# Attention block with adaptive layer norm: the softmax's sums moved from the weights by key to the scores by query, blocks 4 to 15

## The chip, the cores and the metric

The kernel runs on one core of a Trainium2 chip. The metric is the device time of one execution in microseconds; the median of three runs is compared. The core has TensorE (PE, the matrix unit; its weight loads are a row of their own, PEld), VectorE (DVE), ScalarE (ACT), GpSimd (POOL) and SyncE (SP, which issues most DMAs). TensorE writes only to PSUM, eight banks of 512 float32 columns on 128 partitions.

## The reference

Eight sequences of 1024 rows, 512 wide, 16 heads of 32, all float32:

```
mod = silu(condition) @ Wada + bada          # six rows per sequence: shift, scale, gate, twice
xm = layernorm(x) * (1 + sc_a) + sh_a
q, k, v = split(xm @ Wqkv)
attn = softmax(causal(q @ k.T * hd**-0.5))   # sums over the keys
x = x + gt_a * (attn @ v @ Wproj + bproj)
xm = layernorm(x) * (1 + sc_m) + sh_m
x = x + gt_m * (gelu(xm @ W1 + b1) @ W2 + b2)
```

## The kernel before

The rows are cut into 16 blocks of 512, two per sequence: block n has h = n % 2, and the odd block attends to the keys of both. Heads are taken four at a time (a group, g = 0 to 3), one on each quarter of TensorE's rows or columns. The linear products (q, k, v, proj, up, down) use a scheme with seven products of half size for a product of four quarters; their operands' sums and differences run on VectorE and GpSimd.

Attention makes each score twice. **By query** (`scores`, L1828): the scores of a query tile of 128 rows go into the four-bank PSUM tile `sc`, the causal mask is added on VectorE (L1842), and VectorE takes the maximum of each row (L1845). Per group there are whole units of 512 keys and units on the diagonal: one of 512 columns, one of 384 and 128, one of twice 256 that two groups share. `split_maxima` cuts the maxima into three bfloat16 parts, and `maxima_rows` turns them into a row by small matmuls (L1883). **By key** (`weights_T`): the negative maximum (L1909, bfloat16) and the scores (L1921) are added up in the PSUM tile `st`, and ScalarE takes the exponential of 2048 elements at once (L1934) into `pT` in SBUF. `sc` and `st` are the same four banks: one buffer, so each use waits for the one before to be read. Three further banks serve all linear products (`bank`), and the last is `po`, the sum of weights times values (`weigh`, L1962).

The softmax's sums come from the weights by key: `add_weights` (L2047, GpSimd) adds the group's `pT` tiles up, and `finish` multiplies the total by a matrix of ones (L1983, TensorE), which gives each query's sum on all its rows. ScalarE takes the logarithm (L1993), copies `po` (L1996), takes the exponential of the negative logarithm (L2001), and VectorE or GpSimd multiplies.

What stands where in each engine's queue is decided when the program is recorded. A recorder keeps a clock for each engine from planned costs (`note`, `note_pe`, `note_act`) and due times of what is written and read. The linear products are generators; `step_aside` inserts their matmuls ahead of an attention step until the step's buffer is due to be free. `plan` lists the linear steps by window; `MANNER` has leanings for single groups. The chip then runs each queue in that order, with semaphores.

Of the kernel before, what the change touches and what calls it, by code (L numbers as in the profile page):

```python
# [22 lines left out]
def kernel(  # L23
# [252 lines left out]

    plan = {
# [7 lines left out]
    for w in range(1, NB):  # L285
# [167 lines left out]
    cond_act = tmp.tile([P, TB], F32, tag="top", name="cond_act", bufs=1)[:B, :]  # L453
# [939 lines left out]
    def down(n, part):  # L1393
# [77 lines left out]
        def key(kind):  # L1471
            return {"u1": "p1", "u3": "p1", "u5": "u4", "u2": "u2"}.get(kind) or y_key(kind)

        got = partials
        if part == 0:
# [3 lines left out]
            got["u1"] = stage("p1", "p1")  # L1479
# [3 lines left out]
            got["u5"] = stage("p5", "u4")  # L1483
# [23 lines left out]
        else:  # L1507
            u2, u5 = got["u2"], got["u5"]
            bank, ps = yield from product("B11")
            u3 = stage("u3", "p1")  # L1510
# [141 lines left out]
    def work():  # L1652
# [10 lines left out]
        done_linear[0] += spent[0] - before  # L1663
        run_jobs()
# [22 lines left out]
    def step_aside(reads, writes):  # L1687
# [12 lines left out]
        while BANK in writes and bank_at() == NEVER:  # L1700
            work()
        run_jobs()
# [7 lines left out]
    TRIANGLE = [[0], [1, 3], [2]]  # L1710
    MANNER = {(0, 1): (1000, 300), (0, 3): (1000, 300), (1, 3): (-1000, 0), (2, 0): (-1000, 0), (2, 1): (2500, 0), (3, 1): (0, 0), (4, 0): (1000, 300), (6, 0): (1000, 300), (8, 0): (1000, 300), (10, 0): (1000, 300), (12, 1): (2500, 0), (14, 3): (0, 0), (3, 3): (2500, 300)}
# [56 lines left out]

    def scores(n, g, parts):

        h = blocks[n][1]
        for gg in {part[4]: None for part in parts}:
            if (n, gg) not in maxima:
                maxima[n, gg] = small.tile([P, 2, NTT, HPG], F32, tag="mx", name=f"mx_{n}_{gg}")
        reads = [("qT", n), ("kT", n - h + parts[0][1])]
        if (
            linear_wait() > 3000
# [6 lines left out]
        if units[unit_at[0] + 1 :] == [] or units[unit_at[0] + 1][:2] != (n, g):  # L1784
            split_maxima(n, g, h)

    def scores_by_heads(n, g, parts, reads):

        h = blocks[n][1]
        for some in (range(HPG - 1), range(HPG - 1, HPG)):  # L1790
# [14 lines left out]
            for j, bank in of.items():  # L1805
# [8 lines left out]
                for qt, kh, c0, w, gg in parts:  # L1814
# [3 lines left out]
                    note("DVE", 170 + w, [("l", bank)], [("mx", n, gg)])  # L1818
                live[bank] = False

    def scores_at_once(n, g, parts, reads):
# [22 lines left out]
        for qt, kh, c0, w, gg in parts:  # L1844
            nc.vector.tensor_reduce(  # L1845
                maxima[n, gg][:, kh, qt, :], sc[:, :, c0 : c0 + w], axis=AX.X, op=ALU.max
            )
            note("DVE", 170 + 4.14 * w, ["st"], [("mx", n, gg)])

    def split_maxima(n, g, h):  # L1850
# [3 lines left out]
        m = mx[:, 0, :, :]  # L1854
        split = mcols.rearrange("p t (j c) -> p t j c", c=hd)
        high, middle, low = (split[:, :, :, i] for i in range(3))
        rest = small.tile([P, NTT, HPG], F32, tag="rest", name=f"rest_{n}_{g}")
        if h:
# [16 lines left out]
    def maxima_rows():  # L1875
        while rows_due:
# [95 lines left out]
    def finish(n, g):  # L1972

        run_jobs(True)
        acc, slot = totals.pop((n, g))
# [256 lines left out]
```

## Time and profile before

| | us |
|---|---|
| median of 3 runs (3444.2 to 3452.72) | 3445.95 |
| the profiled execution | 3444.65 |
| its span | 3442.9 |
| TensorE busy | 3414.4 |
| VectorE busy | 2070.1 |
| GpSimd busy | 1920.2 |
| ScalarE busy | 1283.6 |

A row of a group reads: line, engine, operation, tile written<-tiles read, shape, count, then busy us, mean ns, and idle time before it with what ended it. Busy times of matmul groups overlap, since matmuls are pipelined; each float32 matmul makes two records. A row of a wait reads: who <- what it waited for, us in all, times, longest. A row of a stage has the engines' busy time in the order TensorE, weight loads, VectorE, ScalarE, GpSimd, then the granted clock, the DMA share and GB/s.

### The profile page before, as it was taken

What the parts mean: (1) busy time and instruction counts of PE and PEld (TensorE: products, weight loads), DVE (VectorE), ACT (ScalarE), POOL (GpSimd) and SP (SyncE); (2) the same over time, 40 slices, a digit from 0 to 9 for tenths busy, and PEclk for the clock granted to TensorE, in tenths of its full rate; (3) what the DMA queues carried; (4) which work ended last, traced back from release to release, by engine and by line L of the source; (5) the groups of instructions that cost most, each with busy time, mean ns of one, the idle gap of its engine ahead of it and who ended that gap; (6) DMA issues with size and microseconds to landing.
All of it is one profiled execution on the core that took longest, in us unless ns stands there. A gap on an engine that the chain in (4) does not pass through costs nothing.

```text
span 3442.9 us, 122860 instructions
## 1 busy us (share of the span) xinstructions
PE 3414.4 (99%) x55594; PEld 1772.7 (51%) x55594; DVE 2070.1 (60%) x2317; ACT 1283.6 (37%) x1418; POOL 1920.2 (56%) x2088
## 2 busy tenths in 40 slices
PE   8999999999999999999999999999999999999999
PEld 5544554455544555455554455454554545545555
DVE  6765666647566475664657546575566756556463
ACT  2345244333243333434344342432524335142431
POOL 3576755756267572675626755377553765447430
PEclk9999999999999999999999999999999999999999
DMA  6842434345544455444544445444464454533444
GB/s 231 279 129 85 119 116 137 102 120 156 170 136 130 129 159 157 133 139 130 167 142 133 136 137 171 136 133 141 129 186 129 126 149 148 167 109 103 121 142 137
DMA packets 380532, 490.69 MB, mean 143 GB/s; under 512 B 28487, under 2 KB 236511, under 8 KB 380010
## 3 DMA queue, kind: packets, MB, share of 16 engines
q1 hardware_dynamic: 379814, 482.54, 46.8%
q8 instruction: 438, 7.18, 0.9%
q14 instruction: 84, 0.69, 0.1%
q10 hardware_dynamic: 196, 0.28, 0.0%
HBM read 429.18 MB, written 53.53 MB: 140 GB/s over the span
## 4 chain that ended last, share of the span: by engine, by line
PE 92%; ACT 3%; DVE 3%; DMA 1%; issue 1%; POOL 1%; SPq 0%; DVEq 0%; ACTq 0%; POOLq 0%
PE bank L233 64%; PE sc L1828 9%; PE po L1962 7%; PE st L1921 7%; PE st L1909 3%; PE bank L1983 2%; DVE mx L1845 1%; ACT pT L1934 1%; ACT hT L1331 1%; PE bank L1883 0%; DMA xm_m<-turned_m 0%; DVE sc L1842 0%; ACT L1331 0%; PE bank L909 0%; ACT L170 0%
## 5 line engine op out<-in xcount | busy, mean ns | idle before, releaser
L2047 POOL TENSOR_TENSOR pT<-pT,pT 128x256 f32<-128x256 f32 (+3 forms) x1254 | 1221.5, 1010 | 173.9 <-ACT pT L1934 136.2
L1934 ACT ACTIVATE pT<-st 128x2048 f32<-128x2048 f32 x288 | 541.2, 1879 | 974.6 <-PE st L1921 884.0
L233 PE MATMUL bank<-w,hT 128*32 128x256 f32 x14336 | 812.9, 380 | 0.0
L1845 DVE TENSOR_REDUCE mx<-sc 128x4 f32<-128x2048 f32 (+3 forms) x384 | 665.6, 1754 | 210.5 <-PE sc L1828 204.3
L233 PEld LDWEIGHTS bank<-w,hT 128*32 128x32 f32 x14336 | 454.3, 110 | 357.0 <-issue 72.3
L233 PE MATMUL bank<-xm_m,w 128*32 128x256 f32 x8192 | 500.2, 380 | 0.8 <-ACT p_u L217 0.8
L233 PE MATMUL bank<-t_m,w 128*32 128x256 f32 x6144 | 381.2, 380 | 0.2
L233 PEld LDWEIGHTS bank<-xm_m,w 128*32 128x32 f32 x8192 | 255.0, 110 | 229.2 <-issue 65.4
L1939 POOL TENSOR_SCALAR_AFFINE_SELECT pT<-pT 128x512 f32<-128x512 f32 x256 | 172.2, 691 | 351.4 <-ACT pT L1934 349.9
L1828 PE MATMUL sc<-kT,qT 32*128 32x512 f32 (+3 forms) x3072 | 329.1, 520 | 1.3 <-DVE mx L1845 1.1
L1842 DVE TENSOR_TENSOR sc<-sc,mask 128x1024 f32<-128x1024 f32 (+1 forms) x160 | 162.8, 1017 | 245.3 <-PE sc L1828 181.5
L1962 PE MATMUL po<-pT,v 128*32 128x512 f32 (+3 forms) x3072 | 304.5, 491 | 0.0
L1921 PE MATMUL st<-qT,kT 32*128 32x512 f32 (+3 forms) x3072 | 300.0, 486 | 0.0
L233 PEld LDWEIGHTS bank<-t_m,w 128*32 128x32 f32 x6144 | 189.8, 110 | 174.7 <-issue 45.6
L233 PE MATMUL bank<-xm_a,w 128*32 128x256 f32 x3968 | 238.8, 380 | 1.7 <-ACT xm_a L924 1.1
L190 POOL TENSOR_TENSOR qT<-top,rec 128x512 f32<-128x512 f32 x58 | 75.4, 1300 | 284.2 <-ACT rec L2001 280.6
L1828 PEld LDWEIGHTS sc<-kT,qT 32*128 32x128 f32 x3072 | 129.4, 183 | 159.6 <-issue 59.2
L222 DVE TENSOR_TENSOR hT<-bank,u_u 128x512 f32<-128x512 f32 x192 | 129.5, 685 | 122.3 <-PE bank L233 119.4
L233 PE MATMUL bank<-w,qT 128*32 128x256 f32 (+1 forms) x3008 | 187.7, 389 | 0.0
L233 PE MATMUL bank<-t_a,w 128*32 128x256 f32 x2944 | 178.8, 380 | 0.5 <-DVE qT L222 0.5
L233 PEld LDWEIGHTS bank<-xm_a,w 128*32 128x32 f32 x3968 | 126.4, 110 | 100.6 <-issue 18.6
L1331 ACT ACTIVATE hT<-hT,cols 128x512 f32<-128x512 f32 x256 | 164.0, 711 | 17.8 <-DVE hT L222 17.1
(251 smaller groups left out, 3393.9 us busy)
## 6 DMA issues: line engine op xcount, KB each, us to landing
w<-in_L_cond_W_dram SPq DMA_DIRECT2D x384, 256.0 KB
w<-kept_up_S SPq DMA_DIRECT2D x256, 256.0 KB
w<-kept_down_S SPq DMA_DIRECT2D x256, 256.0 KB
w<-kept_qkv_S SPq DMA_DIRECT2D x180, 256.0 KB
w<-in_L_cond_Wqkv_dram SPq DMA_DIRECT2D x147, 256.0 KB
hat<-in_x_dram SPq DMA_DIRECT2D x64, 256.0 KB
xr<-in_x_dram SPq DMA_DIRECT2D x64, 256.0 KB
out_dram<-xr SPq DMA_DIRECT2D x64, 256.0 KB
```

The source lines that it names most:

```text
L222: nc.vector.tensor_tensor(out, src, other, op)
L233: nc.tensor.matmul(ps[r], columns, rhs, start=start, stop=stop, skip_group_check=True)
L1331: nc.scalar.activation(hT[:, i, :], hT[:, i, :], AF.Gelu, bias=cols[:, O_B1 + f : O_B1 + f + 1])
L1828: nc.tensor.matmul(sc[:, j, c0 : c0 + w], qTs[n][r, gg, ts(qt, P)], keys_of(n, kh)[r, gg, :w], start=True, stop=True, skip_group_check=True,)
L1842: nc.vector.tensor_tensor(place, place, shape_of.to_broadcast(place.shape), ALU.add)
L1845: nc.vector.tensor_reduce(maxima[n, gg][:, kh, qt, :], sc[:, :, c0 : c0 + w], axis=AX.X, op=ALU.max)
L1909: nc.tensor.matmul(st[:, j, c0 : c0 + w], minus_ones[r, :], row[r, TB - w :], start=(c0 == 0), stop=False, skip_group_check=True,)
L1921: nc.tensor.matmul(st[:, j, c0 : c0 + w], kT[r, gg, ts(k % NTT, P)], qT[r, gg, TB - w :], start=False, stop=True, skip_group_check=True,)
L1934: nc.scalar.activation(pT[:, :, :used], st[:, :, :used], AF.Exp, scale=scale)
L1939: nc.gpsimd.affine_select(diagonal, diagonal, pattern=[[0, HPG], [1, P]], compare_op=ALU.is_ge, fill=0.0, base=0, channel_multiplier=-1,)
L1962: nc.tensor.matmul(po[r, TB - w :], v[:, k % NTT, g * P + j * hd : g * P + (j + 1) * hd], pT[:, j, c0 : c0 + w], start=(k == 0), stop=last ...
L2047: nc.gpsimd.tensor_tensor(into, into, pT[:, j, c0 : c0 + w], ALU.add)
```

## The change

In blocks 4 to 15 the sums are taken where the scores lie by query. After the maximum of a unit (taken two heads at a time where a part is wider than 300 columns), VectorE writes the shift, the maximum times minus the scale. ScalarE then takes, head by head, the exponential of the scores in place in PSUM, with the shift as bias pointer and the row's sum as second output. These run as jobs when the recorder's clock finds the shift written. `split_maxima` adds: in odd blocks the two key halves' sums are brought to one maximum; then the logarithm of the sum, divided by the scale, is added to the maximum. The weights by key so come out normalised. `add_weights`, the ones product, the logarithm of the sums by key, the inversion and the multiplication are left out for these blocks; `po` is copied once. The buffer is free for its next use after the exponentials.

Beside that, the partial tiles of the down products get buffers of their own (in place of `top` and `rec`), and in windows after odd blocks `q` and `k` of the next block stand between the first and the second quarter of the down product. The planned need of a score unit rises from 2100 to 3300 ns per 512 columns. `MANNER` is the same.

```diff
+    def by_logs(n):
+        return n >= 4
...
-            steps = late + head + [("v", w), ("proj", n), ("mt", n)] + downs + [("q", w + 1), ("k", w + 1)]
+            steps = late + head + [("v", w), ("proj", n), ("mt", n)]
+            if even or not by_logs(w + 1):
+                steps += downs + [("q", w + 1), ("k", w + 1)]
+            else:
+                steps += downs[:1] + [("q", w + 1), ("k", w + 1)] + downs[1:]
...
-            got["u1"] = stage("p1", "p1")
+            got["u1"] = stage("p1", "p1d")
...
+    EXP_ACC, HALVE, HEADS_TOO = 170, 300, False
...
+    def run_score_jobs(everything=False):
+        while score_jobs and (everything or due(score_jobs[0][1]) <= max(now["PE"], now["ACT"])):
+            score_jobs.pop(0)[0]()
...
+    def shift_of(n, gg, kh, qt, heads):
+        nc.vector.tensor_scalar(
+            shifts[n, gg][:, kh, qt, heads], maxima[n, gg][:, kh, qt, heads], -scale, None, ALU.mult
+        )
+        note("DVE", 100, [("mx", n, gg)], [("shift", n, gg, kh, qt, heads.start)], port=True)
+
+    def sum_exp(place, n, gg, kh, qt, j, w, reads):
+        exp_table()
+        nc.scalar.activation(
+            place, place, AF.Exp, bias=shifts[n, gg][:, kh, qt, j : j + 1], scale=scale,
+            accum_out=sums_of[n, gg][:, kh, qt, j : j + 1],
+        )
+        note_act(EXP_ACC + 0.84 * w, "exp", reads, [("sums", n, gg)])
+
+    def sum_later(n, some, place, qt, kh, w, gg):
+        shift_of(n, gg, kh, qt, some)
+        key = ("shift", n, gg, kh, qt, some.start)
+
+        def sums():
+            for j in range(some.start, some.stop):
+                sum_exp(place[:, j, :], n, gg, kh, qt, j, w, ["st", key])
+
+        ns = (some.stop - some.start) * (EXP_ACC + 0.84 * w)
+        left["st"] = max(left["st"], now["ACT"], written[key]) + ns
+        written["sums", n, gg] = NEVER
+        score_jobs.append((sums, [key]))
...
         for qt, kh, c0, w, gg in parts:
-            nc.vector.tensor_reduce(
-                maxima[n, gg][:, kh, qt, :], sc[:, :, c0 : c0 + w], axis=AX.X, op=ALU.max
-            )
-            note("DVE", 170 + 4.14 * w, ["st"], [("mx", n, gg)])
+            whole = [slice(0, HPG)]
+            for some in [slice(0, 2), slice(2, HPG)] if w > HALVE and by_logs(n) else whole:
+                nc.vector.tensor_reduce(
+                    maxima[n, gg][:, kh, qt, some], sc[:, some, c0 : c0 + w], axis=AX.X, op=ALU.max
+                )
+                note("DVE", 170 + 1.035 * (some.stop - some.start) * w, ["st"], [("mx", n, gg)])
+                if by_logs(n):
+                    sum_later(n, some, sc[:, :, c0 : c0 + w], qt, kh, w, gg)
...
+        if logs and h:
+            nc.vector.tensor_tensor(rest, m, mx[:, 1, :, :], ALU.max)
+            for kh in range(2):
+                nc.vector.tensor_tensor(shift[:, kh], mx[:, kh], rest, ALU.subtract)
...
+            nc.scalar.activation(shift, shift, AF.Exp, scale=scale)
...
+            nc.vector.tensor_tensor(total, total, shift, ALU.mult)
+            nc.vector.tensor_tensor(total_0, total_0, total[:, 1, :, :], ALU.add)
...
+        if logs:
+            exp_table()
+            nc.scalar.activation(total_0, total_0, AF.Ln)
+            note_act(230, "exp", [("sums", n, g)], [("sums", n, g)])
+            nc.vector.scalar_tensor_tensor(m, total_0, 1.0 / scale, rest if h else m, ALU.mult, ALU.add)
...
+        if by_logs(n):
+            finish_by_logs(n, g)
+            return
...
+    def finish_by_logs(n, g):
+        po, into = outs.pop((n, g)), qTs[n][:, g, :]
...
+        if sooner(["po"], [("att", n)], 600, 585) == "DVE":
+            nc.vector.tensor_copy(into, po)
+            note("DVE", 600, ["po"], [("att", n)])
+        else:
+            nc.scalar.copy(into, po)
+            note_act(585, None, ["po"], [("att", n)])
...
-                if k > 0:
+                if k > 0 and not by_logs(n):
                     add_weights(n, g, [part for part in parts if part[3] == g], pT, slot)
```

TensorE, block 5, first two units of the second group (`sc_5_1_0_0`: block, group, query tile, key half; `bank` rows are linear matmuls). Before:

```order
L1828 MATMUL sc_5_1_0_0_11167<-kT_4_8095,qT_5_10427 128x512 x4
L233 MATMUL bank_2_97<-t_m3_10121,w_335_10863 32x256 x4
L233 MATMUL bank_0_95<-xm_m3_10120,w_337_10918 32x256 x16
L233 MATMUL bank_1_96<-t_m3_10121,w_338_10938 32x256 x4
L1828 MATMUL sc_5_1_1_0_11205<-kT_4_8095,qT_5_10427 128x512 x4
```

The same place of the changed kernel:

```order
L1887 MATMUL sc_5_1_0_0_11112<-kT_4_8081,qT_5_9863 128x512 x4
L233 MATMUL bank_2_97<-t_m3_10263,w_328_10795 32x256 x4
L233 MATMUL bank_1_96<-xm_m3_10262,w_330_10854 32x256 x16
L233 MATMUL bank_0_95<-t_m3_10263,w_331_10881 32x256 x16
L233 MATMUL bank_1_96<-xm_m3_10262,w_332_10929 32x256 x8
L1887 MATMUL sc_5_1_1_0_11182<-kT_4_8081,qT_5_9863 128x512 x4
```

Between the two units there were 24 linear matmuls; now there are 44.

ScalarE at the same place (`mrow` is the row of maxima; `hT` and `p1_u` copies empty a bank; `pT` are weights). Before:

```order
L1889 CAST mrow_5_0_11144<-bank_1_96 128x512
L217 COPY hT_3_2_11056<-bank_0_95 128x2x256
L1331 ACT_TABLE_LOAD
L1331 ACTIVATE hT_3_1_10867<-hT_3_1_10867,cols_169 128x512 x4
L170 ACT_TABLE_LOAD
L1934 ACTIVATE pT_5_0_0_11293<-st_5_0_0_11284 128x2048
```

The changed kernel, from the same row of maxima:

```order
L1974 CAST mrow_5_0_11100<-bank_0_95 128x512
L1796 ACTIVATE sc_5_1_0_0_11112,sums_5_1_10845<-sc_5_1_0_0_11112,shift_5_1_10844 128x512 x2
L217 COPY hT_3_1_10989<-bank_1_96 128x2x256
L1796 ACTIVATE sc_5_1_0_0_11112,sums_5_1_10845<-sc_5_1_0_0_11112,shift_5_1_10844 128x512 x2
L1338 ACT_TABLE_LOAD
L1338 ACTIVATE hT_3_0_10864<-hT_3_0_10864,cols_169 128x512 x4
L170 ACT_TABLE_LOAD
L1796 ACTIVATE sc_5_1_1_0_11182,sums_5_1_10845<-sc_5_1_1_0_11182,shift_5_1_10844 128x512 x4
```

The exponentials over `sc` with their sums (L1796) have come in between copies and gelus.

TensorE at the end of block 5's first group. Before:

```order
L1962 MATMUL po_5_0_11383<-pT_5_0_6_11864,v_5_11582 32x256 x4
L233 MATMUL bank_0_95<-w_360_11686,qT_4_7930 32x256 x12
L233 MATMUL bank_1_96<-w_361_11688,qT_4_7930 32x256 x12
L1983 MATMUL bank_2_97<-pT_5_0_0_11293,ones_158 32x512 x4
L1828 MATMUL sc_5_2_1_0_11991<-kT_4_8095,qT_5_10427 128x512 x4
```

The changed kernel:

```order
L2047 MATMUL po_5_0_11390<-pT_5_0_6_11953,v_5_11632 32x256 x4
L233 MATMUL bank_1_96<-w_362_11798,qT_4_7916 32x256 x16
L1887 MATMUL sc_5_2_1_0_12125<-kT_4_8081,qT_5_9863 128x512 x4
L233 MATMUL bank_2_97<-w_363_11856,qT_4_7916 32x256 x16
L233 MATMUL bank_0_95<-w_364_11893,hT_3_0_10864 32x256 x16
L233 MATMUL bank_0_95<-w_365_11912,hT_3_0_10864 32x256 x16
```

The ones product (L1983) is gone from the end of the group.

More of the change, by code (lines that the diff above doesn't have):

```diff
@@ L2026, in finish @@
             either(qTs[n][:, g, :], top, rec, ALU.mult, [kr, "top"], [("att", n)])
+        if g == NC - 1:
+            written["attended", n] = 0.0
+    def finish_by_logs(n, g):
+        po, into = outs.pop((n, g)), qTs[n][:, g, :]
+        if (n, g) == groups[-1]:
+            for i in range(NTT):
+                some = slice(i * P, (i + 1) * P)
+                if i % 2:
+                    nc.scalar.copy(into[:, some], po[:, some])
+                    note_act(280, None, ["po"], [("att", n, i)])
+                else:
+                    nc.vector.tensor_copy(into[:, some], po[:, some])
+                    note("DVE", 200, ["po"], [("att", n, i)])
+            return
+        if g == 2 and n not in plain_proj:
+            half_sums(n, "T1")
+        if sooner(["po"], [("att", n)], 600, 585) == "DVE":
+            nc.vector.tensor_copy(into, po)
+            note("DVE", 600, ["po"], [("att", n)])
+        else:
+            nc.scalar.copy(into, po)
+            note_act(585, None, ["po"], [("att", n)])
         if g == NC - 1:
@@ L2115, in close @@
             shared[n, g + 1] = other, pT, slot
-        elif parts[0][0] > 0 and (n, g) != first_end:
+        elif by_logs(n) or parts[0][0] > 0 and (n, g) != first_end:
             free_p.append(slot)
         if parts[0][0] == 0:
-            totals[n, g] = (pT, slot)
+            if not by_logs(n):
+                totals[n, g] = (pT, slot)
             if (n, g) in shared:
```

60 lines of the change are left out of this document (47 added, 13 removed).

## The prediction

> **What bounds the kernel now.** I read the page's engine totals and slices first, then the busy time by stage, then who waits for whom on TensorE. The stages are cut at 0, 300, 900 and 3290 us; the scores of block 4 start at about 700 us.
>
> ```profile
> span 3442.9 us, 122860 instructions
> PE 3414.4 (99%) x55594; PEld 1772.7 (51%) x55594; DVE 2070.1 (60%) x2317; ACT 1283.6 (37%) x1418; POOL 1920.2 (56%) x2088
> ...
> PEclk9999999999999999999999999999999999999999
> ```
> ```profile
> 0.00:300.00 300.00, 281.45 (x4385) 148.61 (x4386) 200.44 (x247) 112.15 (x130) 172.32 (x207) 1.00 0.60 195
> ...
> 900.00:3290.00 2390.00, 2386.43 (x38928) 1230.12 (x38924) 1426.17 (x1561) 922.93 (x1002) 1374.00 (x1482) 1.00 0.47 139
> ```
> ```profile
> PE st L1909 <- DVE mx L1845: 5.1, 12, 1.4
> ...
> PE bank L1883 <- POOL mcols L1867: 3.2, 4, 1.6
> ...
> PE sc L1828 <- DVE mx L1845: 1.1, 2, 0.7
> ```
>
> TensorE is the bound. From 900 to 3290 us it is idle for 2390.00 - 2386.43 = 3.6 us, at full granted clock. What the change takes from TensorE is therefore gained in full, and every wait that it gives TensorE is lost in full. What it takes from GpSimd or adds to ScalarE counts only where TensorE comes to wait for it. The few waits there are show where that happens first: at the four-bank score buffer (`sc` and `st` share it), which VectorE or ScalarE must leave before the next scores can be written.
>
> **The gain: 48 ones products.** A ones product is 8 records (each float32 matmul is recorded twice). Its price is the step from its start to the next start, since matmuls overlap.
>
> ```profile
> L1983 PE MATMUL bank<-pT,ones 128*32 128x512 f32 (+3 forms) x536 | 69.1, 583 | 0.0
> L233 PE MATMUL bank<-w,hT 128*32 128x256 f32 x14336 | 812.9, 380 | 0.0
> ```
> ```profile
> 3295.76 1.91 PE L233 MATMUL bank<-w,hT 128*32 128x256 f32 x32
> 3297.49 1.04 PE L1983 MATMUL bank<-pT,ones 128*32 128x512 f32 x8
> 3298.35 1.03 PE L233 MATMUL bank<-w,hT 128*32 128x256 f32 x13
> ```
>
> The step is 3298.35 - 3297.49 = 0.86 us; the bar is 1.04. Blocks 4 to 15 have 48 groups: 48 x 0.86 = 41 us, or 50 us by the bars. I take 41, the step, because the next matmul overlaps the bar's end.
>
> Off the path: 946 of the 1254 GpSimd additions go, and 48 logarithms and inversions with their multiplications.
>
> ```profile
> L2047 POOL TENSOR_TENSOR pT<-pT,pT 128x256 f32<-128x256 f32 (+3 forms) x1254 | 1221.5, 1010 | 173.9 <-ACT pT L1934 136.2
> ```
>
> That is 946 x 1.010 = 955 us of GpSimd work, hidden behind TensorE, which waited for GpSimd only the 3.2 us above. I give it nothing, as I do the separate buffers of the down products and the new place of `q` and `k` in the plan: TensorE has no wait there to lose. The tail keeps its matmuls and is full of them. GpSimd's shorter queue can only make VectorE's small operations steadier, which bounds the 0.2 us used below.
>
> **The price: the score buffer is held longer.** The change adds 1152 exponentials (576 of 512 columns, 192 each of 384, 256 and 128), in place over the scores, each with a pointer for its bias and a sum as second output. No row has that form. The nearest:
>
> ```profile
> L1993 ACT ACTIVATE rec<-bank 128x512 f32<-128x512 f32 x64 | 38.1, 595 | 125.2 <-PE bank L1983 125.1
> L726 ACT ACTIVATE rstd_m<-mv_m,eps 128x4 f32<-128x4 f32 x15 | 4.4, 294 | 0.0
> L727 ACT ACTIVATE rstd_m<-rstd_m 128x4 f32<-128x4 f32 x15 | 3.1, 205 | 0.5
> L1934 ACT ACTIVATE pT<-st 128x2048 f32<-128x2048 f32 x288 | 541.2, 1879 | 974.6 <-PE st L1921 884.0 <-POOL pT L2047 45.8 <-POOL mcols L1866 20.1
> ```
> ```profile
> 209.85 0.29 ACT L726 ACTIVATE rstd_m<-mv_m,eps 128x4 f32<-128x4 f32 x1
> 210.17 0.21 ACT L727 ACTIVATE rstd_m<-rstd_m 128x4 f32<-128x4 f32 x1
> ...
> 1571.31 2.56 ACT L1331 ACTIVATE hT<-hT,cols 128x512 f32<-128x512 f32 x4
> ```
>
> A pass from PSUM over 512 columns takes 595 ns, a bias pointer adds 294 - 205 = 89 (a column costs (1879 - 595)/1536 = 0.84 ns, by L1934 over 2048). In the built order 843 of the 1152 wait for the ScalarE instruction just ahead of them, as L727 waits for L726: L727 starts 0.32 us after L726, which takes 0.29, so such a wait adds 0.03. Together 0.71 us at 512 columns: 0.29 fixed and the columns' share. From below: four gelus with the same pointer and no wait take 2.56 us, 0.62 each in step. From above: if the sum is read out by an instruction of its own, as small as L727's 205 ns, 0.71 + 0.20 = 0.91. I take 0.71, since the row nearest in form has every part but the sum. The Trainium skill ("ScalarE: Activation LUTs", What ACT_TABLE_LOAD costs) has back-to-back ACTIVATEs overlap by about 93 ns; the gelus here do that, L726 and L727, which wait, do not. By that rule alone each would cost 0.62 us, and the waits below would be some 14 us fewer.
>
> VectorE's part, by shape:
>
> ```profile
> L1842 DVE TENSOR_TENSOR sc<-sc,mask 128x1024 f32<-128x1024 f32 x96 | 118.1, 1230 | 127.3 <-PE sc L1828 91.2 <-issue 16.1 <-ACT top L1996 12.1
> L1845 DVE TENSOR_REDUCE mx<-sc 128x4 f32<-128x1536 f32 x64 | 112.5, 1757 | 2.2
> L1845 DVE TENSOR_REDUCE mx<-sc 128x4 f32<-128x1024 f32 x64 | 75.4, 1219 | 1.1
> L1842 DVE TENSOR_TENSOR sc<-sc,mask 128x512 f32<-128x512 f32 x64 | 44.7, 698 | 118.0 <-PE sc L1828 90.3 <-ACT hat L736 21.6 <-issue 6.1
> L718 DVE BATCH_NORM_AGGREGATE mv_m<-st_m 128x2 f32<-128x6 f32 x60 | 10.9, 182 | 2.1
> L1859 DVE TENSOR_TENSOR mx<-mx 128x16 f32<-128x16 f32 x32 | 12.8, 399 | 0.6
> ```
>
> From the last score matmul to a free buffer, then. A whole unit: maximum of two heads 1.22, shift 0.2 (182 ns is the nearest small row, 399 the upper one), four exponentials 4 x 0.71, the second half's maximum beside the first two, handing over 0.2: 4.5 us. A diagonal unit of 512 columns adds the mask, 0.70 and some: 5.3. The unit of 384 and 128: mask 1.23, half of 1.76, 0.2, then 4 x 0.61 + 4 x 0.39: 6.7. The unit of 256 and 256: mask 1.23, maximum 1.22, 0.2, 8 x 0.50: 7.0.
>
> Against this stands the TensorE work that the new order puts behind each unit, priced at 812.9/7168 = 0.113 us a matmul (the row of 14336 records is 7168 matmuls). Of the two TensorE places shown with the change, the first is a whole unit of block 5. Behind it 24 linear matmuls have become 44, so 2.7 us have become 5.0, against a need of 4.5. I counted all 216 units of blocks 4 to 15, need against cover. The 96 whole units are all covered. Of the 48 diagonal ones of 512 columns 2 are not, in blocks 12 and 14, where only 1.8 us stand behind them: 7 us. Of the 48 of 384 and 128 columns 8 fall short, 4 us in sum; of the 24 of twice 256, 17, 12 us. Together 23 us at 0.71 an exponential; 9 at 0.62; 134 at 0.91; and with 0.4 for the shift 36. The same count on the kernel before gives 8 us where the rows show some 6, so it is a usable one.
>
> ScalarE's queue, shown for the same place, holds what this count leaves out: bank copies now stand behind exponentials that wait for VectorE, and exponentials behind gelus. The recorder's plan has room for 600 ns an exponential (`EXP_ACC`, 170 + 0.84 x 512), 0.11 under my price. What the queue adds beyond the count I put at 3 us, and the longer way from the last sum through logarithm and split to the rows of maxima (7.8 us of cover at the least, for 6.7 and some 2 of small operations) at 2.
>
> Sum: -41 + 23 + 3 + 2 = -13. The profiled execution took 3444.65 us around its span of 3442.9, 1.3 under the median of 3445.95; on the median's scale 3433.
>
> **Rivals.** First, slower: the sum output costs an instruction of its own. The exponential is then 0.82 to 0.91 us (the 205 ns, with or without the 0.09 by which gelus overlap); at 0.82 the same count gives waits of 63 us, at 0.91 134: 3446 - 41 + 63 or 134, 3468 to 3539. It decides against the change from about 0.76 us an exponential. For it speaks that no row shows a sum output for nothing; against it, nothing in the trace. The Trainium skill ("VectorE: DVE Perf Modes", Two Vector instructions with no wait between them) says of VectorE that an operation which also writes out its accumulator is two instructions; no run here shows whether ScalarE does so.
>
> Second, slower: the banks. Three banks serve all linear products, and 182 bank copies stay on ScalarE. If each of the 156 units of odd blocks delays one copy by one exponential's half, TensorE waits 156 x 0.35 = 55 us: 3460. Against it: those copies had slack before.
>
> ```profile
> ACT p_u L217 <- PE bank L233: 256.3, 39, 11.8
> ```
>
> ScalarE waited for TensorE 256 us ahead of 39 of them, not TensorE for ScalarE.
>
> Third, faster: the covers hold almost everywhere, at 0.62 us an exponential or with VectorE quicker than I take it; waits of 9 us at most: 3446 - 41 + 9 = 3414, and 3400 at the very best.
>
> **How the numbers follow.** My forecast, -13 with an own range of 3420 to 3445, has 0.38; the sum's own instruction 0.30; the banks 0.10; the covers holding 0.22. A difference under 0.3% (10 us) can't be told from none. The forecast case is 0.25 faster, 0.12 same and 0.01 slower; the third rival all faster; the two slower rivals 0.02 same, the rest slower. So faster 0.47, same 0.14, slower 0.39. The range goes from 3403, which leaves 0.05 below, to 3490, which leaves about 0.13 of the first rival above.
>
> **What would show it.** No L1983 counterpart after block 3. A mean of the new exponentials near 680 to 710 ns, and no instruction of another name behind each; a step of 0.71. TensorE's waits led by `sc` and `st` for ScalarE, some 30 us in all, with the units of twice 256 columns worst. GpSimd near 970 us. If TensorE waits for ScalarE by over 60 us, the price of the exponential is what I had wrong; if its `bank` waits grow, the banks.

## The result and the profile after

The changed kernel takes 3778.55 us at the median of four runs (3772.38 to 3784.11), beside 3445.73 us of the kernel before, timed with it: 1.0964 times the time, with a 95% interval of 1.0951 to 1.0977. It is 333 us slower. The forecast was 3433 us with a range to 3490.

The profiled execution took 3784.11 us. The head of its page and one stage, the same stage as the one shown of before:

```profile
span 3782.3 us, 124226 instructions
PE 3444.1 (91%) x55210; PEld 1784.9 (47%) x55210; DVE 2083.8 (55%) x3047; ACT 1983.5 (52%) x3658; POOL 1080.8 (29%) x1202
PE 54%; ACT 22%; DVE 17%; issue 5%; DMA 1%; POOL 1%; SPq 0%; ACTq 0%; DVEq 0%; POOLq 0%
```
```profile
900.00:3290.00 2390.00, 2129.44 (x34188) 1101.72 (x34184) 1290.59 (x2031) 1382.68 (x2741) 522.03 (x572) 0.98 0.42 126
```

No engine is near full but TensorE, and TensorE now stands still: 260.6 us in this stage where it stood still 3.6, and 338 us in the whole span where it was 28.5. In the chain that ended last (the third line) ScalarE and VectorE hold 39%. Who made TensorE wait, and for what ScalarE itself waited:

```profile
PE st L1994 <- ACT sc L1796: 206.2, 145, 4.1
PE sc L1887 <- ACT sc L1796: 49.4, 44, 2.6
PE bank L233 <- DVE u_v L222: 10.6, 5, 2.1
PE bank L233 <- ACT p_u L217: 8.4, 10, 1.5
PE sc L1887 <- ACT pT L2019: 8.2, 6, 1.7
PE bank L233 <- DVE t_a L941: 6.6, 2, 3.3
```
```profile
ACT sc L1796 <- DVE mx L1906: 651.4, 181, 10.1
```

The first two rows are the score buffer waiting for the new exponentials (L1796): 255.6 us. Their groups, and one whole unit in the order of time:

```profile
L1796 ACT ACTIVATE sc<-sc,shift 128x512 f32<-128x512 f32 x576 | 381.6, 662 | 479.8 <-DVE mx L1906 443.6 <-PE bank L233 23.4
L1796 ACT ACTIVATION_READ_ACCUMULATOR sc<-sc,shift 128x1 f32 x1152 | 222.9, 193 | 0.0
```
```profile
2013.84 1.14 PE L1887 MATMUL sc<-kT,qT 32*128 32x512 f32 x8 [1.26 <-ACT sc L1796]
...
2015.05 1.23 DVE L1906 TENSOR_REDUCE mx<-sc 128x2 f32<-128x1024 f32 x1 [0.45 <-PE sc L1887]
2016.31 0.17 DVE L1789 TENSOR_SCALAR shift<-mx 128x2 f32<-128x2 f32 x1
2016.38 1.22 DVE L1906 TENSOR_REDUCE mx<-sc 128x2 f32<-128x1024 f32 x1
...
2017.71 0.66 ACT L1796 ACTIVATE sc<-sc,shift 128x512 f32<-128x512 f32 x1 [3.93 <-DVE mx L1906]
...
2018.30 0.19 ACT L1796 ACTIVATION_READ_ACCUMULATOR sc<-sc,shift 128x1 f32 x1
2018.53 0.66 ACT L1796 ACTIVATE sc<-sc,shift 128x512 f32<-128x512 f32 x1
```

Two things are to be seen here. Behind each exponential stands a second instruction that reads out the sum; the step from one exponential to the next is 2018.53 - 2017.71 = 0.82 us, and over the four of this unit 0.81. And the first exponential begins only when the second half's maximum is done (2016.38 + 1.22 = 2017.60), although its own shift was there at 2016.48. The halves do not overlap. In none of the 96 whole units does the first exponential start before the second maximum has ended; the earliest is 0.09 us behind it.

Put into the prediction's own count over the 216 units, the two corrections give this: the fixed part of a step is 0.385 us (0.81 less 512 columns at 0.84 ns), and the second half's maximum and shift come ahead of all exponentials. A whole unit then holds the buffer for 6.2 us instead of 4.5; 68 of the 96 whole units and 101 of the other 120 fall short of cover, by 255 us in sum. The rows above show 255.6, and in the trace the 96 whole units take 6.2 us on the mean from the end of the last score matmul to the end of the last exponential, before handing over. With the read-out alone the same count gives 60 us, with the lost overlap alone 170. The experiments try these numbers.

### The profile page after: what moved, and what is told of

Same layout as the page of the kernel before. It is cut to its first block, busy times and chain, and to the rows that moved or that the text cites. A ratio compares the mean times of both kernels' runs of the same rounds, so it can differ in the third digit from the quotient of the medians.

```text
span 3782.3 us, 124226 instructions
## 1 busy us (share of the span) xinstructions
PE 3444.1 (91%) x55210; PEld 1784.9 (47%) x55210; DVE 2083.8 (55%) x3047; ACT 1983.5 (52%) x3658; POOL 1080.8 (29%) x1202
## 4 chain that ended last, share of the span: by engine, by line
PE 54%; ACT 22%; DVE 17%; issue 5%; DMA 1%; POOL 1%; SPq 0%; ACTq 0%; DVEq 0%; POOLq 0%
PE bank L233 30%; ACT sc L1796 15%; DVE mx L1906 11%; PE sc L1887 7%; PE st L2006 7%; PE po L2047 6%; DVE sc L1901 3%; PE st L1994 3%; ACT hT L1338 2%; ACT pT L2019 2%; DVE shift L1789 2%; ACT L1338 1%; ACT L170 1%; PE bank L1968 0%; PE bank L2071 0%
## 5 line engine op out<-in xcount | busy, mean ns | idle before, releaser
L1796 ACT ACTIVATE sc<-sc,shift 128x512 f32<-128x512 f32 (+3 forms) x1152 | 639.9, 555 | 715.8 <-DVE mx L1906 651.4
L1906 DVE TENSOR_REDUCE mx<-sc 128x2 f32<-128x1024 f32 (+5 forms) x576 | 700.7, 1220 | 227.4 <-PE sc L1887 221.6
L1887 PE MATMUL sc<-kT,qT 32*128 32x512 f32 (+3 forms) x3072 | 330.3, 522 | 58.3 <-ACT sc L1796 49.4
L2006 PE MATMUL st<-qT,kT 32*128 32x512 f32 (+3 forms) x3072 | 316.2, 506 | 0.0
L2158 POOL TENSOR_TENSOR pT<-pT,pT 128x512 f32<-128x512 f32 (+3 forms) x308 | 295.9, 996 | 53.4 <-ACT pT L2019 37.4
L1994 PE MATMUL st<-mrow,minus_ones 32*128 32x512 bf16 (+3 forms) x1536 | 116.4, 334 | 209.9 <-ACT sc L1796 206.2
L1796 ACT ACTIVATION_READ_ACCUMULATOR sc<-sc,shift 128x1 f32 x1152 | 222.9, 193 | 0.0
L1948 POOL CAST mcols<-mx 128x16 bf16<-128x16 f32 x63 | 17.6, 279 | 695.5 <-DVE mx L1940 644.7
L233 PE MATMUL bank<-t_a,w 128*32 128x256 f32 x2944 | 187.9, 385 | 14.7 <-DVE t_a L941 6.6
```

The lines of the kernel that those rows point to most:

```text
L233: nc.tensor.matmul(ps[r], columns, rhs, start=start, stop=stop, skip_group_check=True)
L1796: nc.scalar.activation(place, place, AF.Exp, bias=shifts[n, gg][:, kh, qt, j : j + 1], scale=scale, accum_out=sums_of[n, gg][:, kh, qt, j ...
L1887: nc.tensor.matmul(sc[:, j, c0 : c0 + w], qTs[n][r, gg, ts(qt, P)], keys_of(n, kh)[r, gg, :w], start=True, stop=True, skip_group_check=True,)
L1906: nc.vector.tensor_reduce(maxima[n, gg][:, kh, qt, some], sc[:, some, c0 : c0 + w], axis=AX.X, op=ALU.max)
L1994: nc.tensor.matmul(st[:, j, c0 : c0 + w], minus_ones[r, :], row[r, TB - w :], start=(c0 == 0), stop=False, skip_group_check=True,)
L2006: nc.tensor.matmul(st[:, j, c0 : c0 + w], kT[r, gg, ts(k % NTT, P)], qT[r, gg, TB - w :], start=False, stop=True, skip_group_check=True,)
```

## The experiments

Each run is compared with the kernel before as timed on its own chip (3446.33 to 3454.74 us). All but one are single runs. On one chip the kernel before took 3451.4 us in a single run and 3446.33 at the median of seven, and the kernel with two tiles stands 137 us over it in one comparison and 147 in another. So the differences are good to about 10 us, an estimate from these two pairs.

**Without the exponentials.** TensorE's order stays as it is.

```diff
-        nc.scalar.activation(
-            place, place, AF.Exp, bias=shifts[n, gg][:, kh, qt, j : j + 1], scale=scale,
-            accum_out=sums_of[n, gg][:, kh, qt, j : j + 1],
-        )
...
+                    nc.gpsimd.memset(sums_of[n, gg], 1.0)
```

> Left out: the 1152 exponentials over the scores; the sums they would give are set to one by GpSimd. The order on TensorE and VectorE is that of the changed kernel, instruction for instruction. Theory A, the score buffer is held too long by the exponentials: the 256 us that TensorE waits for them go, TensorE idles under 40 us, the granted clock is 1.00 again, and with 48 ones products gone (41 us) the time is 3395 to 3425 us. Theory B, the new order of TensorE's work (fewer products between units, work on banks in other places) costs by itself: the bank waits of some 50 us stay and the time is 3440 to 3480 us.

Measured: 3446.58 us, 8 us under its kernel before (3454.74).

```profile
PE 3382.7 (98%) x55210; PEld 1767.1 (51%) x55210; DVE 2094.2 (61%) x3047; ACT 1228.8 (36%) x1354; POOL 1092.4 (32%) x1250
```
```profile
PE bank L233 <- DVE u_v L222: 10.6, 5, 2.1
PE sc L1884 <- ACT pT L2016: 10.2, 7, 1.8
PE bank L233 <- DVE t_a L941: 7.5, 3, 3.3
```

All waits for L1796 are gone. From the changed kernel's profiled execution to this one the span falls by 3782.3 - 3444.9 = 337 us, of which 276 are idle time of TensorE and 61 are busy time. The exponentials make the loss. But the time lies in theory B's range, and TensorE still idles for 3444.9 - 3382.7 = 62 us, not under 40. The new order without any exponential gains only 8 us: it has waits of its own, in the rows above at the changes from one pair of blocks to the next. So A holds for the large part, and B for some 20 us (the gain is measured below).

**Without the sum output.**

```diff
             place, place, AF.Exp, bias=shifts[n, gg][:, kh, qt, j : j + 1], scale=scale,
-            accum_out=sums_of[n, gg][:, kh, qt, j : j + 1],
...
+                    nc.gpsimd.memset(sums_of[n, gg], 1.0)
```

> Left out: the sum output of the 1152 exponentials (the exponentials run, the sums are set to one by GpSimd). The order on TensorE, VectorE and ScalarE is that of the changed kernel. Theory A: the second instruction behind each exponential goes, the step of four exponentials of 512 columns falls from 0.81 us to 0.69 to 0.73 us, a buffer is held 0.4 us less, and by my count of hold against cover over the 216 units the waits for ScalarE fall from 256 us to 150 to 190 us: 3680 to 3720 us. Theory C, the second instruction runs beside the next exponential and costs nothing of its own: the step stays above 0.78 us and the time within 20 us of 3784 us.

Measured: 3644.7 us, 190 over its kernel before. The read-out instruction is gone; four exponentials take 2.75 us, so that the step is (2.75 - 0.66)/3 = 0.70 us. The exponential itself is as long as ever:

```profile
L1796 ACT ACTIVATE sc<-sc,shift 128x512 f32<-128x512 f32 x576 | 381.5, 662 | 481.8 <-DVE mx L1906 464.3 <-PE bank L233 4.6
```
```profile
1407.20 2.75 ACT L1796 ACTIVATE sc<-sc,shift 128x512 f32<-128x512 f32 x4
```
```profile
PE st L1994 <- ACT sc L1796: 124.0, 130, 3.2
PE sc L1887 <- ACT sc L1796: 25.5, 37, 1.7
```

C falls. The waits are 149.5 us, at the lower edge of what A expects. The time fell by 139 us, more than A's 60 to 100, for 106 us less of waits: each microsecond of wait costs more than itself. The section on the prediction says where the rest is.

**Two tiles for a unit.** In the changed kernel the first exponential waits for the second maximum though they touch different banks; both refer to the one tile of four banks. Here the four banks are two tiles of two heads.

```diff
-        sc = ps_st.tile([P, HPG, TB], F32, tag="st", name=f"sc_{n}_{g}_{parts[0][0]}_{parts[0][1]}")
+        sc = [
+            ps_st.tile([P, 2, TB], F32, tag=f"st{i}", name=f"sc{i}_{n}_{g}_{parts[0][0]}_{parts[0][1]}")
+            for i in range(2)
+        ]
...
-                    sc[:, j, c0 : c0 + w],
+                    sc[j // 2][:, j % 2, c0 : c0 + w],
...
-        nc.scalar.activation(pT[:, :, :used], st[:, :, :used], AF.Exp, scale=scale)
+        for i, half in enumerate(st):
+            nc.scalar.activation(pT[:, 2 * i : 2 * i + 2, :used], half[:, :, :used], AF.Exp, scale=scale)
```

> The four banks of a unit are taken as two tiles of two heads instead of one tile of four; so each reduce and each exponential of a unit refers to the tile of its own two heads. The exponential of the weights and the mask become two instructions each, the maxima of parts up to 256 columns too. The order on TensorE is that of the changed kernel but for 12 instructions at the start. Theory A (both failed terms count: the sum read-out and the lost overlap of the halves): the first exponential starts during the second half's maximum, the hold of a whole unit falls by about 1.1 us, and the waits for ScalarE fall from 256 us to 60 to 110 us (60 by my count, and up to 50 for 0.2 us more on each weights unit): 3590 to 3640 us. Theory D, the halves do not matter since ScalarE is the engine that limits the unit: under 40 us gained, 3745 us or more.

> The kernel with the units as two tiles again, all work kept, timed in three rounds: 3585 to 3600 us and a ratio to the kernel before of 1.038 to 1.044. Theory A has the halves' overlap worth 190 us of the 339 us lost; the rival that the first look of it was a chance of its chip would show a ratio above 1.05.

Measured: 3591.97 us in a single run, 137 over its kernel before. Timed: 3593.77 us (3588.63 to 3595.35) beside 3446.33, a ratio of 1.0424 with an interval of 1.0407 to 1.0442. A whole unit, and the waits, of the first of the two runs:

```profile
2019.83 0.17 DVE L1790 TENSOR_SCALAR shift<-mx 128x2 f32<-128x2 f32 x1
2019.90 1.22 DVE L1912 TENSOR_REDUCE mx<-sc 128x2 f32<-128x1024 f32 x1
2020.11 0.66 ACT L1797 ACTIVATE sc<-sc,shift 128x512 f32<-128x512 f32 x1 [2.90 <-DVE shift L1790]
```
```profile
PE st L2002 <- ACT sc L1797: 68.8, 94, 3.6
PE sc L1891 <- ACT sc L1797: 4.9, 10, 1.2
```

The first exponential now starts 0.1 us behind its shift, beside the second maximum. In 88 of the 96 whole units it starts before the second maximum has ended, and the time from the last score matmul to the last exponential falls from 6.2 to 5.2 us. The waits are 73.7 us, where the count had 60, and 186 to 196 of the 333 us come back, net of what the form itself costs (below). D and the chance of a chip fall. Nearly all of the waits that are left stand behind the narrower units: counted by the unit ahead of the wait, the changed kernel has 109.8 us behind units of 512 columns, 99.6 behind those of 384 and 128 and 46.3 behind those of twice 256; two tiles have 1.9, 52.8 and 19.0. This is the fastest of the kernels here that leave nothing out of the change, and still slower than the kernel before.

**Both together: near to the kernel as the prediction costed it.** Two tiles, and no sum output (the two diffs above).

> Left out: the sum output of the 1152 exponentials (sums set to one). With the units as two tiles of two heads as well, this is the kernel as the prediction costed it: halves overlap, a step of 0.71 us. TensorE's order is that of the changed kernel but for 12 instructions at the start. Theory A (the two terms are all that was missed in the hold of the buffer): waits for ScalarE 20 to 50 us, the run of the two tiles less 70 to 100 us, 3490 to 3520 us. Theory G (the hold has a third part that neither names): waits above 60 us and 3540 us or more.

Measured: 3507.99 us, 57 over its kernel before; waits for ScalarE at the score buffer 29.8 us.

```profile
PE st L2002 <- ACT sc L1797: 29.0, 60, 3.0
```

G falls by its bounds, and the count of the prediction had 23 us for just this. But the halves overlap only in units of 512 columns. All of the 29.8 us stand behind the narrower ones (23.9 behind 384 and 128, 5.9 behind twice 256). One of 384 and 128:

```profile
2025.82 1.15 PE L1891 MATMUL sc<-kT,qT 32*128 32x384 f32 x16
2029.26 0.17 DVE L1790 TENSOR_SCALAR shift<-mx 128x2 f32<-128x2 f32 x1
2030.40 0.75 DVE L1912 TENSOR_REDUCE mx<-sc 128x2 f32<-128x256 f32 x2
2030.91 3.46 ACT L1797 ACTIVATE sc<-sc,shift 128x384 f32<-128x384 f32 x8
```

The shift of the first two heads is there at 2029.43, and their exponentials begin at 2030.91, when both halves' maxima of 384 columns and the first of the part of 128 are done; that part lies in the same tiles. In all 48 such units the first exponential starts at least 0.56 us after the second half's maximum, on the mean 4.6 us after the last score matmul, where the prediction has 2.3 (mask, half a maximum, shift).

So the read-out and the single tile, above all by the lost overlap in units of 512 columns, explain 276 of the 333 us, and their shares depend on the order in which they are taken away: the read-out is worth 143 us with the halves apart and 81 with them overlapping, the two tiles 133 or 196.

**What is left of the 57 us.** Two tiles without any exponential over the scores (the first diff above and the one of the two tiles):

> The kernel with units of two tiles of two heads, the exponentials over the scores left out (sums set to one); TensorE's order is that of the two-tile runs. It divides the 61 us that the run with two tiles and without the sum output stands above the run without exponentials. If the exponentials, costed as the prediction had them (halves overlapping, 0.71 us a step), still make those 61 us, this run is at 3440 to 3465 us. If the two-tile form itself makes them (heads of a unit that start one pair after the other, two instructions for each exponential of the weights), it is at 3490 to 3510 us.

Measured: 3459.88 us, 14 over its kernel before. Exponentials at the costed price still make 57 - 14 = 43 us, or 48 us by the plain difference of the two runs. The form of two tiles makes 14 + 8 = 22 us against the run with one tile and no exponentials, or 13 us by the plain difference. The two ways differ because the kernel before took 3454.74 us beside the one run and 3446.33 beside the other.

**The gain alone.** The kernel before without the 48 ones products:

```diff
-            for j in range(HPG):
+            for j in range(HPG if n < 4 else 0):
...
-        nc.scalar.activation(rec, banks[bank], AF.Ln)
+        if n < 4:
+            nc.scalar.activation(rec, banks[bank], AF.Ln)
+        else:
+            nc.scalar.activation(rec, outs[n, g], AF.Copy, scale=0.0)
```

> The kernel before, with the 48 ones products of blocks 4 to 15 left out and nothing else moved: the reciprocals are of one, the weights' additions on GpSimd stay. It measures the gain term alone. Predicted 41 us: 3400 to 3410 us by the raw length of the products. If their ends lie under the next matmuls, 28 to 35 us: 3412 to 3420 us.

Measured: 3422.44 us, 29 under its kernel before (3451.4), and 24 under the median of seven runs of it on the same chip.

```profile
PE 3376.2 (99%) x55210; PEld 1764.1 (52%) x55210; DVE 2074.7 (61%) x2317; ACT 1280.6 (37%) x1418; POOL 1916.3 (56%) x2088
```
```profile
PE sc L1828 <- ACT pT L1934: 6.9, 12, 0.7
PE st L1909 <- ACT pT L1934: 4.3, 7, 0.8
```

TensorE's busy time falls by 3414.4 - 3376.2 = 38 us. Its idle time rises from 28.5 to 44.5: the products had been cover for the weights' exponential (both rows; the kernel before has 0.3 us of such waits), which TensorE now reaches before it is done. The difference is that of the second expectation, but not by its reason: most of the products' length is gone from the busy time, and the loss is new idle time.

**The planner told the true price.** One number for the fixed part of the exponential, and maxima of a unit in one:

```diff
-    EXP_ACC, HALVE, HEADS_TOO = 170, 300, False
+    EXP_ACC, HALVE, HEADS_TOO = 385, 1000, False
```

> The same work with the planner's price of an exponential's fixed part at 385 ns instead of 170 ns, as measured, and maxima of a unit in one instruction instead of halves. Theory E, the loss is the planner's wrong price (linear work is there, but put elsewhere): waits for ScalarE fall under 120 us, 3580 to 3650 us. Theory F, the one score buffer is too short of time: each pair of blocks needs about 416 us of buffer time against 415 us of TensorE's work, so that a better order finds no cover: 3700 us or more.

Measured: 3741.4 us, 287 over its kernel before. E falls. F's bound is met, but the run does not show F's reason. Against the changed kernel TensorE is idle for 302 us instead of 338, in fewer and longer waits:

```profile
PE st L1994 <- ACT sc L1796: 176.1, 50, 8.9
PE sc L1887 <- ACT pT L2019: 47.6, 19, 7.2
```

**Two tiles and the true price, all widths by halves.**

```diff
-    EXP_ACC, HALVE, HEADS_TOO = 170, 300, False
+    EXP_ACC, HALVE, HEADS_TOO = 385, 300, False
...
-        for qt, kh, c0, w, gg in parts:
-            whole = [slice(0, HPG)]
-            for some in [slice(0, 2), slice(2, HPG)] if w > HALVE and by_logs(n) else whole:
+        for i, half in enumerate(sc):
+            some = slice(2 * i, 2 * i + 2)
+            for qt, kh, c0, w, gg in parts:
```

> Nothing left out: two tiles of two heads for every unit, the maxima of all widths by halves, and the planner told of 385 ns of fixed time an exponential and of the second instruction for the weights. If hold against cover sets the time (theory A), all units gain by the overlap, not only those of 384 and 512 columns, and the planner puts more cover where it is needed: 3500 to 3570 us. If the buffer's total time is what binds (theory F), it stays within 30 us of the run with the two tiles, 3560 to 3620 us.

Measured: 3646.27 us, 195 over its kernel before, worse than either theory expects and than the two tiles alone. The waits at the score buffer for ScalarE are 84 us (58.4 for L1797 in 27 waits of up to 9.2, 25.7 for the weights), where two tiles alone have 78 by the same rows; new waits of 15.8 us for `v` stand beside them, and the granted clock is 0.974 instead of 0.992. Why this plan has them was not settled.

**The planner's share for a unit**, on the two tiles:

```diff
-        ns = 300 + sum(100 + (3300 if by_logs(n) else 2100) * w / TB for _, _, _, w, _ in parts)
+        ns = 300 + sum(100 + (4700 if by_logs(n) else 2100) * w / TB for _, _, _, w, _ in parts)
```

> The kernel with units of two tiles, all work kept, with the planner's share of linear work for a unit of scores raised from 3300 to 4700, about what the buffer is held; 560 of TensorE's instructions stand elsewhere. If the 74 us of waits come from too small a share behind the units of scores, they fall under 45 us and the time to 3530 to 3565 us. If linear work is bound where it stands by its own operands, little moves: 3580 to 3610 us.

Measured: 3593.48 us, with 72.4 us of waits. The linear work behind a unit does not follow that number.

**The waits at the pairs of blocks.** Three tries to find what makes the 21 us by which the new order falls behind (8 gained instead of 29, each good to about 10), all without exponentials over the scores and each with one of these edits:

```diff
-                if previous is not None and (g, k) == (0, 0) and by_logs(n):
-                    close(*previous)
-                    previous = None
-                    for i in (n, n + 1) if h == 0 else (n,):
-                        written["free for v", i] = 0.0
```
```diff
-            if even or not by_logs(w + 1):
-                steps += downs + [("q", w + 1), ("k", w + 1)]
-            else:
-                steps += downs[:1] + [("q", w + 1), ("k", w + 1)] + downs[1:]
+            steps += downs + [("q", w + 1), ("k", w + 1)]
```
```diff
-        ns = 300 + sum(100 + (3300 if by_logs(n) else 2100) * w / TB for _, _, _, w, _ in parts)
+        ns = 300 + sum(100 + 2100 * w / TB for _, _, _, w, _ in parts)
```

> The kernel without the exponentials over the scores (left out, sums set to one), and with the last weighted sum of a block closed behind the next block's first weights, as the kernel before does, instead of ahead of them. If the early close is what makes TensorE wait some 5 us at each pair of blocks (for the products' sums u_v, the weights pT, the columns t_a), the time falls by 15 to 30 us against the run without the exponentials, to 3417 to 3432 us. If those waits come from the order of the down products and the next columns instead, it stays within 8 us of 3446.6 us.

> The kernel without the exponentials over the scores (left out, sums set to one), with the next pair's columns of q and k behind all four down products again, as the kernel before orders them, instead of behind the first. If that reordering makes the 30 us of waits at the five pairs of blocks (u_v 10.6 us, weights pT 10.2 us, t_a 7.5 us) that the kernel before has not, the time falls from 3446.6 us to 3415 to 3430 us. If those waits come from elsewhere in the new order, it stays within 8 us of 3446.6 us or rises.

> The kernel without the exponentials over the scores (left out, sums set to one), with the planner's share of linear work for a unit of scores at 2100 again in place of 3300; 620 of TensorE's 31527 instructions stand elsewhere. If that share makes the 30 us of waits at the pairs of blocks, the time falls from 3446.6 us to 3415 to 3432 us; if not, it stays within 8 us.

Measured: 3455.16 us (4 over its kernel before, where the run without exponentials is 8 under), 3520.91 us (75 over), 3448.79 us (3 under). None brings the time down; the second is far worse, with 48.1 us in which the score buffer waits for VectorE's maxima:

```profile
PE st L1988 <- DVE mx L1900: 48.1, 16, 4.3
```

So the moved columns are of use to the new order. The early close seems to be of use too, by 12 us, which is near the noise, and the planner's share shows nothing. What makes the waits at the pairs of blocks stays open. Whether the buffers of the down products do it was not tried.

## Why the prediction was wrong

**The step that failed most** is "the second half's maximum beside the first two" in the need of a whole unit, 4.5 us. The halves came one after the other. In the trace the first exponential of a unit waits for the second maximum. That was not among the rivals, and no row of before could show it. The prediction took from the built order which exponentials wait for the instruction ahead on their own engine, and did not ask for which VectorE instruction the first one waits. By the runs two tiles are worth 133 to 196 us; of 109.8 us of waits behind units of 512 columns they leave 1.9. The same step failed in the unit of 384 and 128 columns: by its terms the exponentials begin 2.3 us after the last score matmul, in the trace 4.8 us after it on the mean, and two tiles bring that only to 4.6.

**The step that was mis-sized** is the price of the exponential, 0.71 us at 512 columns: it measures 0.81. Without the sum output the step is 0.70, so the rest of the price was right in sum. The first rival named the part, a read-out instruction of its own, with 0.205 us from a small row; it is 0.193, and 0.11 in step, since it starts 0.07 us before the exponential's end. The rival had a chance of 0.30 and 3468 us at 0.82. A kernel with that price and with overlapping halves takes 3592 us, so the rival's time was too low as well.

**The count of hold against cover** was of use. With the corrected steps it has 255 us where 255.6 were measured; that this agrees to a microsecond is luck, since for the three experiments it has 170, 60 and 23 where 149.5, 73.7 and 29.8 were. The last two of these are also too low as measured: with two tiles some of the wait is hidden in the busy time (last section). The needs of 6.7 and 7.0 us for the narrower units are 0.1 to 0.2 above the sums of the terms listed for them.

**"Every wait that it gives TensorE is lost in full"** was too little. Against the run without exponentials the changed kernel loses 337 us for 255.6 us of waits. TensorE's busy time, with the same matmuls in the same order, is 3444.1 - 3382.7 = 61 us longer. Most of that, 43 us, is the clock:

```profile
788.33 1.50 PE L233 MATMUL bank<-t_m,w 128*32 128x256 f32 x24 [0.69 <-DVE hT L222]
792.30 0.40 PE L1994 MATMUL st<-mrow,minus_ones 32*128 32x384 bf16 x8 [2.46 <-ACT sc L1796]
792.51 1.99 PE L2006 MATMUL st<-qT,kT 32*128 32x384 f32 x16
```
```profile
791.00:792.00 1.00, 0.00 (x0) 0.00 (x0) 0.00 (x0) 0.94 (x5) 0.00 (x0) 1.00 0.39 112
792.00:793.00 1.00, 0.70 (x12) 0.58 (x15) 0.17 (x1) 0.46 (x3) 0.23 (x1) 0.79 0.25 98
793.00:794.00 1.00, 1.00 (x12) 0.57 (x8) 0.00 (x0) 0.00 (x0) 0.76 (x4) 0.50 0.26 101
...
795.00:796.00 1.00, 1.00 (x28) 0.65 (x24) 0.42 (x1) 1.00 (x1) 0.00 (x0) 0.50 0.06 16
796.00:797.00 1.00, 1.00 (x24) 0.54 (x20) 0.27 (x1) 1.00 (x2) 0.49 (x1) 1.00 0.41 41
```

The number before the DMA share is the granted clock. After a wait of 2.46 us it is 0.50 for 3.4 us, and the score matmuls of this unit take 1.99 us; one of the same shape at full clock takes 1.10:

```profile
954.47 1.10 PE L2006 MATMUL st<-qT,kT 32*128 32x384 f32 x16
```
Cut into slices of 1 us from 700 us to the end, the changed kernel has 26 such spells, 102 us at half clock; TensorE's busy time in them times the missing half is 48 us. Each of these spells lasts 3.41 us or twice that. Without exponentials there are 4 spells and 5 us lost to them, in the kernel before none. What makes the other 18 us of busy time was not found. The trace agrees with what the Trainium skill says ("TensorE: Matmul & The Clock Gate", HAM oscillation — how this bites in real kernels): repeated waits of the engine throttle it again and again, and the price is half of the throttled time. It does not agree on the length: the page's example has waits that cross a window of over 3.4 us, and here one of 2.46 us, with one of 0.69 us shortly before, was enough.

**The gain of 41 us** is 38 us of busy time and 24 to 29 us of time, since the products were cover: what is taken from TensorE is not gained in full.

**What was given nothing** (GpSimd's additions, the down products' buffers, the new places in the plan) costs: the new order without the exponentials gains 8 us where the products alone gain 29. "TensorE has no wait there to lose" was read from the old order, and the new one is another. The additions themselves were hidden, as said: TensorE waits 9.7 us for GpSimd in the changed kernel (4.0, 3.9 and 1.8), none of it for an addition of weights.

**The queue's 3 us and the maxima rows' 2:** TensorE waits 19.1 us for ScalarE's bank copies (8.4 for `p_u`, 3.7 each for `kT` and `qT`, 3.3 for `hT`), against 55 in the second rival, and 3.9 us for the split of the maxima (3.2 before). The second rival did not come.

**What would show it:** no other instruction behind each exponential, wrong; GpSimd near 970 us, measured 1080.8; waits of some 30 us, measured 255.6; the units of twice 256 columns worst, measured 1.9 us of wait for each of them and 2.1 for each of 384 and 128. "If TensorE waits for ScalarE by over 60 us, the price of the exponential is what I had wrong" names only half of the cause.

Even the kernel nearest to the costed one is 57 us slower than before, not 13 faster. Against the run without exponentials and with two tiles it is 43 to 48 us for 29.8 of listed waits. The rest is the 14 us at which that run itself stands: the gain of 29 against the order's 21 and the two tiles' 22, each good to about 10.

## What to carry to other kernels

Price a second output by looking for the instruction that delivers it, and where no row shows one, give the dearer case more than a third. Before two steps are counted as beside each other, read in the built order what the later one waits for: a tile of several banks can be one thing to whoever sets the waits, and two smaller tiles brought back more than half of the loss here. Then read every shape by itself: in the narrower units the two tiles left half of the waits. A wait of a few microseconds on TensorE costs its length and then the half-clock matmuls behind it: here 48 us on top of 338 us of idle time.

## What the runs showed beside this

- Long waits and the half clock: with the planner told the true price, the waits in front of the score buffer are 232 us (176.1, 47.6, 7.0 and 1.5) where the changed kernel has 264 (206.2, 49.4 and 8.2), yet the slices of 1 us show 230 us at half clock instead of 102. Only 110 us of them are busy time of TensorE, so they cost 55 us, against 48 in the changed kernel; the rest falls into time in which TensorE stands still. One wait of that run:

```profile
1249.53 1.15 PE L1887 MATMUL sc<-kT,qT 32*128 32x256 f32 x16 [1.06 <-ACT pT L2019]
1259.54 0.61 PE L1994 MATMUL st<-mrow,minus_ones 32*128 32x512 bf16 x4 [8.87 <-ACT sc L1796]
1259.92 1.94 PE L2006 MATMUL st<-qT,kT 32*128 32x512 f32 x8
```
```profile
1252.00:1253.00 1.00, 0.00 (x0) 0.00 (x0) 0.96 (x2) 0.00 (x0) 0.00 (x0) 1.00 0.26 98
1253.00:1254.00 1.00, 0.00 (x0) 0.00 (x0) 0.96 (x3) 0.00 (x0) 0.00 (x0) 0.77 0.03 12
...
1262.00:1263.00 1.00, 1.00 (x20) 0.38 (x16) 0.00 (x0) 1.00 (x1) 0.00 (x0) 0.50 0.00 0
1263.00:1264.00 1.00, 1.00 (x12) 0.05 (x8) 0.00 (x0) 1.00 (x2) 0.12 (x1) 0.61 0.00 0
```

  The clock fell about 3 us into the wait and came back some 4 us after its end.

- Taking cover away can cost without any added work: without the ones products TensorE waits 6.9 us for the weights' exponential in front of the scores (`sc`), where the kernel before has no such wait.

- With two tiles the heads of a unit start a pair at a time, and part of the wait is hidden in the busy time: the matmuls of L2002 (`st` from the rows of maxima) are busy for 149.1 us with the exponentials, 133.0 with those without a sum output and 116.9 without any.
